# Other order and pace of the weight look-ups, half of the late reloads on GpSimd's queue, later copies of the mirrored Gram blocks

## The chip, the cores and the metric

The kernel runs on one core of one Trainium2 chip, as one launch. The metric is the device time of that launch in microseconds (us). The core has a matrix engine (TensorE, PE in the profile, with its weight loads as PEld), a vector engine (VectorE, DVE), a scalar engine (ScalarE, ACT), GpSimd (POOL) and a queue engine (SyncE, SP). SP and POOL issue the DMA transfers in this kernel.

## What is computed

The input x is 2 x 2048 x 512 in float32. Two layers follow each other, each with a layer norm ahead and the input added behind. In the attention the scores are 512 x 512: the features of q against the features of k, summed over the sequence. The second layer is a gated network whose three weight matrices are given as indices (0 to 15) into a table of 16 numbers.

```python
def attn(x, Wq, Wk, Wv, Wo):
    q, k, v = (einsum('bse,ef->bsf', x, W) for W in (Wq, Wk, Wv))
    s = einsum('bes,bfs->bef', qT, kT) / sqrt(16)
    return swapaxes(einsum('bef,bfs->bes', softmax(s), vT), 1, 2) @ Wo

def ffn(x, lut, gate_idx, up_idx, down_idx):       # 1376 x 512, 1376 x 512, 512 x 1376
    h = silu(x @ lut[gate_idx].T) * (x @ lut[up_idx].T)
    return h @ lut[down_idx].T

x = x + attn(layernorm(x), Wq, Wk, Wv, Wo)
x = x + ffn(layernorm(x), lut, gate_idx, up_idx, down_idx)
```

## The kernel before

The 4096 rows of x are eight chunks c of 512 rows, four chunks for each of the two batches; a chunk has four blocks j of 128 rows. The attention is not computed row by row: since q, k and v are linear in the normed rows n, everything comes from the Gram matrix n^T n of each batch (512 x 512). The stages, with the lines of the profile:

- **Gram stage** (`gram`, L371). For each block, ACT writes the normed rows xn (L183), and PE adds their upper Gram blocks in four banks gp. Blocks are also stored in DRAM as nd, by SP. Batch 0 ends with chunk 3. `gram_out` copies its banks to SBUF at c=4, j=1, and `gram_mirror` fills the lower blocks at c=4, j=3: six PE transposes (L432) into three banks gt, each bank followed by an ACT copy (L435). The sums of the first matrix (`left(gs[0])`) are queued in `ahead` and made by DVE from c=6 on.
- **Square stage** (L516). Products of 512 x 512 matrices, each by a Strassen-like scheme of seven half-size products, give a matrix m for each batch. The second Gram matrix is mirrored inside the first of these products.
- **y stage** (L680). For each of 32 blocks k: SP reloads nd as nl (L657), DVE transposes it 32 x 32 within rows (nT, L661), PE multiplies it by m, DVE adds the result to x (L687), ACT forms sums for the second layer norm and, six blocks later, the normed block xn_f. In block k DVE makes nT of block k+1. For blocks below 16 PE transposes xn_f (L712) to xb. The blocks from 16 on go out to DRAM (xnd, L701), come back as fl in four transfers of 64 KB by `reload` (L657), and are transposed by DVE (L661). `f_load(k)` issues the reload, `f_turned_late(k)` the transpose; they stand two blocks apart, the last of them in the next stage.
- **Gate and up stage** (L808, class `GateUp`). The hidden units are 11 tiles f of 128; the rows are four pairs p of chunks. A pass (f, p) is seven half-size products on PE, in the order a1, c1, a4 of the pass before, a2, c2, b, a3, each of four matmul records (1.72 us at full clock). DVE makes five instructions in a pass, of about 0.69 us (L128, L866, L875); SP stores each h in DRAM (hd, L831). After each of the seven products comes `between()`: it runs one item of the list `todo` (in f=0 the 20 items of late reloads, transposes and sums of xb, `f_sums`, L125), or else `pump(0.9)`.
- **Down stage** (L808, class `Down`): the same scheme with the down weights, then the sum with x and the output.

**The look-ups** are DVE work of a different kind, which the other stages carry along. There is one job for each tile f of gate and up (gu0 to gu10) and one for each two tiles of the down weights (wd0 to wd5). A job takes indices of 128 x 1024 from DRAM (`fetch`; POOL's queue from the third job on), has ACT cast them (L204), takes the bits apart (L216 to L222), and picks: eight instructions L230 and seven copy_predicated L242. A gu job ends with four sums on 128 x 256. Jobs run in one order, the list `jobs`; their index buffers are two, so the fetch of the job after next is let go by the end of a job. A gate holds job gu f (f above 1) until tile f-2 is complete. `pump(us)` adds `us` to an account and runs steps of the current job, at costs written in the code, until the account is used up:

```python
owed[0] = min(owed[0] + us, 2 * us + 1.0)
while owed[0] > 0:
    cost = next(lookup, None)
    if cost is None:
        return
    owed[0] -= cost
```

The costs of the planner are close to the profile's durations: 0.75 for L230, 1.27 for L242. At the head of tile f, whatever is missing of gu f is run at once (called a forced step in the text below):

```python
for f in range(NFT):
    while "S4" not in gu[f]:
        next(lookup)
```

The order on every engine is written out by hand (a manual schedule): an engine executes its instructions in the order in which the program emits them, and waits by semaphores.

Of the kernel before, what the change touches and what calls it, by code (L numbers as in the profile page):

```python
# [51 lines left out]
P = 128  # L52
# [6 lines left out]
def tile_attn_ffn(  # L59
# [13 lines left out]
    nc = tc.nc  # L73
# [4 lines left out]
    J = 4  # L78
    CH = J * P
    NCH = B * S // CH  # L80
    CPB = S // CH
# [3 lines left out]
    NFT = len(FT)  # L85
    NPAIR = NFT // 2
    assert E == 512 and NLUT == 16 and S % CH == 0 and NFT == 2 * NPAIR + 1
    assert B == 2 and NCH == 8
    Q = 32
# [19 lines left out]
    nd = dram.tile([NCH, J, P, E], F32, tag="nd", name="nd")  # L109
    xnd = dram.tile([NCH, J, P, E], F32, tag="xnd", name="xnd")  # L110
# [13 lines left out]
    def sub(dest, a, b):  # L124
        nc.vector.tensor_tensor(dest, a, b, ALU.subtract)  # L125

    def add(dest, a, b):
        nc.vector.tensor_tensor(dest, a, b, ALU.add)  # L128
# [122 lines left out]
    def gu_job(f):  # L251
        f0, rows = FT[f]
        n = KB * rows

        def load(queue, idx):
            queue.dma_start(idx[:, :n], gate_idx[:, KB * f0 : KB * f0 + n])
            queue.dma_start(idx[:, n:], up_idx[:, KB * f0 : KB * f0 + n])

        def dest():
            gu[f] = {  # L260
                "w": wgu.tile([P, 2, KB, P], F32, tag="w", name=f"w_{f}"),
                "s": wgu.tile([P, 3, 2, P], F32, tag="s", name=f"s_{f}"),
            }
            flat = gu[f]["w"].rearrange("p g k r -> p (g k r)")[:, : 2 * n]
            gu[f]["flat"] = flat
            return flat

        def after():
            flat = gu[f]["flat"].rearrange("p (g k r) -> p g k r", g=2, k=KB)
            a11, a12 = flat[:, 0, 0:2, :], flat[:, 0, 2:4, :]  # L270
            a21, a22 = flat[:, 1, 0:2, :], flat[:, 1, 2:4, :]
            s1, s2, s4 = (gu[f]["s"][:, q, :, :rows] for q in range(3))
            for op, d, u, v in (
                (add, s1, a21, a22), (sub, s2, s1, a11), (sub, a21, a11, a21), (sub, s4, a12, s2)
            ):
                op(d, u, v)
                yield 0.42
            gu[f].update(
                {"11": a11, "12": a12, "S3": a21, "22": a22, "S1": s1, "S2": s2, "S4": s4}
            )  # L280

        return Job(f"gu{f}", P, 2 * n, load, dest, after, lambda: f < 2 + passed[0])

    def down_job(i):
        f0, rows = FT[2 * i]
        n = 2 if i < NPAIR else 1

        def load(queue, idx):
            queue.dma_start(
                idx.rearrange("p (o e) -> p o e", o=n),  # L290
                down_idx[f0 : f0 + n * rows, :].rearrange("(o p) e -> p o e", o=n),
            )

        def dest():
            return wd[:rows, 2 * i : 2 * i + n, :].rearrange("p o e -> p (o e)")

        return Job(f"wd{i}", rows, n * E, load, dest, lambda: iter(()), lambda: True)

    jobs = [gu_job(0), gu_job(1)] + [down_job(i) for i in range(NPAIR - 1)]
    jobs += [gu_job(2), gu_job(3), down_job(NPAIR - 1), gu_job(4), gu_job(5), down_job(NPAIR)]  # L300
    jobs += [gu_job(f) for f in range(6, NFT)]

    def looked_up():

# [15 lines left out]
    def pump(us):  # L320
# [7 lines that stand above are left out]
# [26 lines left out]
    def bank(name):  # L354
        return pps.tile([P, E], F32, tag="ps", name=name, bufs=8)
# [7 lines left out]
    def gram(c, j):  # L363
        b = c // CPB
        if c % CPB == 0 and j == 0:
            gp[b] = [bank(f"gp_{b}_{i}") for i in range(KB)]
        xn = ln1[c].normed(j, xc[c][:, j, :])
        if c >= STORED:
            nc.sync.dma_start(nd[c, j], xn)
        for i in range(KB):  # L370
            nc.tensor.matmul(  # L371
                gp[b][i][:, i * P :], xn[:, i * P : (i + 1) * P], xn[:, i * P :],
                start=c % CPB == 0 and j == 0, stop=c % CPB == CPB - 1 and j == J - 1,
            )
# [11 lines left out]
    def left(t, name, order=("S2", "S4", "S1")):  # L386
        a11, a21 = t[:, 0:2, :H], t[:, 0:2, H:]
        a12, a22 = t[:, 2:4, :H], t[:, 2:4, H:]

        def s3():  # L390
            for tag in order:
                o.new(tag)
            sub(a21, a11, a21)
            o.update({"11": a11, "12": a12, "22": a22, "S3": a21})

        o = Operand(name, [
            s3, lambda: sub(o["S2"], a22, a21), lambda: sub(o["S4"], a12, o["S2"]),
            lambda: add(o["S1"], o["S2"], a11),
        ])
        return o  # L400
# [17 lines left out]
    gs = {}  # L418

    def gram_out(b):  # L420

        gs[b] = room(f"sq{b}", f"g_{b}")
        for i in range(KB):
            nc.scalar.copy(gs[b][:, i, i * P :], gp[b][i][:, i * P :])

    def gram_mirror(b):

        g = gs[b]
        for m in range(1, KB):
            ps = bank(f"gt_{b}_{m}")  # L430
            for i in range(m):
                nc.tensor.transpose(  # L432
                    ps[:, i * P : (i + 1) * P], g[:, i, m * P : (m + 1) * P], ident
                )
            nc.scalar.copy(g[:, m, : m * P], ps[:, : m * P])  # L435

    def stats1(c, *js):
        for j in js:
# [24 lines left out]
    def n_stored():  # L463
        c, j = to_store.pop(0)
        t = sums.tile([P, E], F32, tag="e", name=f"n_{c}_{j}")
        nc.sync.dma_start(nd[c, j], ln1[c].normed(j, xc[c][:, j, :], t))

    for c in range(1, NCH):
        for j in range(J):
            gram(c, j)  # L470
            if c in (CPB - 1, CPB + 1, CPB + 2):
                n_stored()
            if c + 1 < NCH and j < 2:
                for i in (2 * j, 2 * j + 1):
                    ln1[c + 1].stats(i, xc[c + 1][:, i, :])
                if j == 1:
                    ln1[c + 1].sqrt(0, J)
            elif c + 1 < NCH and j == 2:
                pump(0.6)
                ln1[c + 1].rest(0, J)  # L480
                pump(0.6)
            elif ahead and c > STORED + 2:
                for op in ahead[:4]:
                    op()
                del ahead[:4]
            else:
                pump(1.9)
            if c == 1 and j == 2:
                nc.vector.tensor_tensor(
                    lut_x, lut_pairs[:, :, 0], lut_pairs[:, :, 1], ALU.bitwise_xor  # L490
                )
            if c == CPB and j == 1:
                gram_out(0)
            if c == CPB + 1 and j == 3:
                wk_sb = load_weight(wk, "a0", "wk_sb")
                wq_sb = load_weight(wq, "a1", "wq_sb")
                wk_ops = right(wk_sb, "wk")
                ahead += wk_ops.todo
            if c == CPB and j == 3:
                gram_mirror(0)  # L500
                g_ops = [left(gs[0], "g_0")]
                ahead += g_ops[0].todo

# [67 lines left out]
    class Softmax:  # L571
# [27 lines left out]

    gram_out(1)  # L600
    g = [g_ops[0], left(gs[1], "g_1")]
    wq_ops = left(wq_sb, "wq", ("S2", "S1", "S4"))
    p1 = [room(f"a{2 + b}", f"p1_{b}") for b in range(B)]
    p1_ops = [right(p1[b], f"p1_{b}") for b in range(B)]
    assert not ahead
    square(g[0], wk_ops, p1[0], "p1_0", {
        1: [lambda: gram_mirror(1)], 4: g[1].todo[:2], 5: g[1].todo[2:],
    }, (1.2, 1.2, 1.2, 1.2, 0.3, 0.3, 1.2))
    square(g[1], wk_ops, p1[1], "p1_1", {
        3: wq_ops.todo[:2], 4: wq_ops.todo[2:], 5: p1_ops[0].todo[:2], 6: p1_ops[0].todo[2:],  # L610
# [35 lines left out]
    nls, nTs, ys, xfs, fls = {}, {}, {}, {}, {}  # L646
# [2 lines left out]
    def block(k):  # L649
        return xc[k // J][:, k % J, :]  # L650

    def reload(t, rows):

        rows = rows.rearrange("(t b) e -> b t e", b=Q)
        t = t.rearrange("p (t e) -> p t e", e=P)
        for i in range(KB):
            nc.sync.dma_start(t[i * Q : (i + 1) * Q], rows[:, :, i * P : (i + 1) * P])  # L657

    def turn(to, t):

# [5 lines left out]
    def n_load(k):  # L666
        if k < NBLK:
            nls[k] = sums.tile([P, E], F32, tag="e", name=f"nl_{k}")
            reload(nls[k], nd[k // J, k % J])

    def n_turned(k):
        if k < NBLK:
# [22 lines left out]
    EARLY = NBLK // 2  # L695
# [20 lines left out]

    def f_load(k):
        fls[k] = xnp.tile([P, E], F32, tag="xn", name=f"fl_{k}", bufs=4)
        reload(fls[k], xnd[k // J, k % J])

    def f_turned_late(k):
        turn(f_place(k), fls[k])
# [59 lines left out]
    for k in range(NBLK):  # L782
        if k:
            n_turned(k + 1)
            n_load(k + 3)
        y_product(k)
        if k == 0:
            before[0].a4()
            n_turned(1)
            n_load(2)  # L790
            n_load(3)
        else:
            side(k)
        pump(1.0 if k < EARLY + 6 else 0.5)
    pps.release()
    sums.release()
    ffn = tc.alloc_tile_pool(name="ffn", bufs=1, reuse_waits="tile")
# [319 lines left out]
    for c in range(NCH):  # L1117
        nxt = None
        for jj in range(2):
# [9 lines left out]
            u = units.pop(0)  # L1129
# [62 lines left out]
```

## Time and profile before

| | |
|---|---|
| median of 3 runs | 1124.98 us (1124.23 to 1125.58) |
| profiled execution | 1127.84 us |
| its span | 1125.7 us |
| PE busy | 1095.9 us, 97% |
| DVE busy | 696.3 us, 62% |
| ACT busy | 303.6 us, 27% |
| mean granted clock of PE | 0.991 |

The span is the profiled part of the execution; the rest of the 1127.84 us lies around it. Busy PE is not PE at its peak, since ends of matmuls are modelled. A wait is given as waiting engine and line, then what released it, then total, times and longest in us. In the timeline a line has its start, its length, the engine, the line of the kernel, the operation, and in brackets the idle time of that engine ahead of it. SPq and POOLq are the queues' own instructions.

### The profile page before, as it was taken

What the parts mean: (1) busy time and instruction counts of PE and PEld (TensorE: products, weight loads), DVE (VectorE), ACT (ScalarE), POOL (GpSimd) and SP (SyncE); (2) the same over time, 40 slices, a digit from 0 to 9 for tenths busy, and PEclk for the clock granted to TensorE, in tenths of its full rate; (3) what the DMA queues carried; (4) which work ended last, traced back from release to release, by engine and by line L of the source; (5) the groups of instructions that cost most, each with busy time, mean ns of one, the idle gap of its engine ahead of it and who ended that gap; (6) DMA issues with size and microseconds to landing.
All of it is one profiled execution on the core that took longest, in us unless ns stands there. A gap on an engine that the chain in (4) does not pass through costs nothing.

```text
span 1125.7 us, 10379 instructions
## 1 busy us (share of the span) xinstructions
PE 1095.9 (97%) x3516; PEld 656.0 (58%) x3516; DVE 696.3 (62%) x1267; ACT 303.6 (27%) x567; POOL 14.6 (1%) x31
## 2 busy tenths in 40 slices
PE   7999999999989969999999999999999999999998
PEld 4668886444434424444444444444437888888887
DVE  6887776677677778786876665855553344333341
ACT  4552522556622212222222222222221000000000
POOL 0000000000000000000000000000000000000000
PEclk9999999999999989998999999999999999999999
DMA  8371303545741111110211211101315453355420
GB/s 335 132 262 29 66 19 104 158 132 166 253 142 65 57 47 66 56 54 28 73 60 56 73 38 57 51 37 47 138 54 168 148 168 99 123 173 166 152 71 37
DMA packets 83700, 117.15 MB, mean 104 GB/s; under 512 B 16432, under 2 KB 41008, under 8 KB 81728
## 3 DMA queue, kind: packets, MB, share of 16 engines
q1 hardware_dynamic: 81456, 109.09, 28.9%
q0 software_dynamic: 2192, 7.41, 2.2%
q8 instruction: 27, 0.44, 0.2%
q14 instruction: 25, 0.20, 0.1%
HBM read 64.56 MB, written 51.90 MB: 103 GB/s over the span
## 4 chain that ended last, share of the span: by engine, by line
PE 93%; DVE 3%; SPq 1%; ACT 1%; DMA 1%; issue 1%; DVEq 0%; ACTq 0%
PE a_g L808 25%; PE a_d L808 14%; PE c_g L808 13%; PE y L680 10%; PE c_d L808 7%; PE gp L371 6%; PE b_g L808 6%; PE b_d L808 4%; PE ea_t L516 1%; SPq L657 1%; PE ea_p L516 1%; PE ea_m L516 1%; PE ea_s L516 1%; PE xt L712 1%; PE ec_t L516 1%
## 5 line engine op out<-in xcount | busy, mean ns | idle before, releaser
L128 DVE TENSOR_TENSOR c<-c_g,u 128x512 f32<-128x512 f32 (+1 forms) x44 | 30.3, 689 | 145.0 <-PE c_g L808 138.1
L680 PE MATMUL y<-m,nT 128*128 128x512 f32 x256 | 112.8, 592 | 0.0
L808 PE MATMUL a_g<-xb,w 128*128 128x512 f32 (+1 forms) x176 | 86.5, 615 | 11.8 <-DVE w L242 11.8
L808 PE MATMUL c_g<-xb,w 128*128 128x512 f32 (+1 forms) x176 | 87.0, 619 | 2.3 <-DVE xb L125 2.3
L808 PE MATMUL a_g<-xb,s 128*128 128x512 f32 (+1 forms) x176 | 82.9, 593 | 2.1 <-DVE c L128 2.1
L808 PE MATMUL a_g<-xT_a,s 128*128 128x512 f32 (+1 forms) x176 | 82.8, 593 | 0.1
L808 PE MATMUL b_g<-xb,w 128*128 128x512 f32 (+1 forms) x176 | 82.7, 592 | 0.0
L371 PE MATMUL gp<-xn_a 128*128 128x512 f32 (+3 forms) x256 | 72.6, 447 | 8.5 <-ACT xn_a L183 8.5
L680 PEld LDWEIGHTS y<-m,nT 128*128 128x128 f32 x256 | 47.4, 190 | 52.7 <-issue 52.4
L860 ACT ACTIVATE h<-h 128x512 f32<-128x512 f32 (+1 forms) x44 | 27.7, 631 | 172.8 <-DVE h L128 172.8
L808 PEld LDWEIGHTS a_g<-xb,w 128*128 128x128 f32 (+1 forms) x176 | 33.8, 194 | 56.2 <-issue 42.7
L371 PEld LDWEIGHTS gp<-xn_a 128*128 128x128 f32 x256 | 45.2, 197 | 35.7 <-issue 17.0
L808 PEld LDWEIGHTS c_g<-xb,w 128*128 128x128 f32 (+1 forms) x176 | 34.4, 196 | 48.3 <-issue 43.3
L808 PE MATMUL a_g<-xT_sq,s 128*128 128x512 f32 (+1 forms) x132 | 62.0, 592 | 0.0
L808 PEld LDWEIGHTS a_g<-xb,s 128*128 128x128 f32 (+1 forms) x176 | 33.1, 189 | 46.3 <-issue 39.0
L230 DVE TENSOR_SCALAR gu<-idx_gu,lut_x,lut_sb 128x1024 int32<-128x1024 int32 (+1 forms) x77 | 59.2, 791 | 0.0
L808 PEld LDWEIGHTS a_g<-xT_a,s 128*128 128x128 f32 (+1 forms) x176 | 32.9, 188 | 43.0 <-issue 42.0
L808 PEld LDWEIGHTS b_g<-xb,w 128*128 128x128 f32 (+1 forms) x176 | 33.0, 188 | 42.5 <-issue 42.5
L242 DVE COPY_PREDICATED gu<-b_gu,gu 128x1024 f32<-128x1024 int16 (+1 forms) x44 | 56.4, 1281 | 0.9
L808 PE MATMUL a_d<-dT,hs_a 128*128 128x256 f32 x224 | 56.2, 378 | 0.0
L242 DVE COPY_PREDICATED wd<-b_wd,wd 128x1024 f32<-128x1024 int16 (+1 forms) x42 | 50.9, 1212 | 0.8
L837 ACT COPY p<-a_g 128x512 f32<-128x512 f32 (+1 forms) x44 | 25.7, 584 | 86.0 <-PE a_g L808 86.0
(239 smaller groups left out, 1708.3 us busy)
## 6 DMA issues: line engine op xcount, KB each, us to landing
hd<-h SPq DMA_DIRECT2D x80, 256.0 KB, 2.0
h<-hd SPq DMA_DIRECT2D x40, 512.0 KB, 6.3
nl<-nd SPq DMA_DIRECT2D x128, 64.0 KB, 2.1
x1d<-x SPq DMA_DIRECT2D x8, 1024.0 KB, 4.5
r<-x1d SPq DMA_DIRECT2D x32, 256.0 KB, 4.4
out_dram<-r SPq DMA_DIRECT2D x32, 256.0 KB, 2.5
x<-in_x_dram SPq DMA_DIRECT2D x7, 1024.0 KB, 14.3
nd<-xn_a SPq DMA_DIRECT2D x20, 256.0 KB, 2.1
```

What stands on the lines that cost most here:

```text
L128: nc.vector.tensor_tensor(dest, a, b, ALU.add)
L230: vec.tensor_scalar(dest.bitcast(I32), idx, lut_x[:rows, k : k + 1], lut_i[:rows, at : at + 1], ALU.bitwise_and, ALU.bitwise_xor,)
L242: vec.copy_predicated(dest, masks[level - 1], t)
L371: nc.tensor.matmul(gp[b][i][:, i * P :], xn[:, i * P : (i + 1) * P], xn[:, i * P :], start=c % CPB == 0 and j == 0, stop=c % CPB == CPB - ...
L516: nc.tensor.matmul(ps[:, m, :], self.a[a][:, k, m * P : (m + 1) * P], self.b[b][:, k, :], start=first and m == k == 0, stop=k == 1, skip_g ...
L657: nc.sync.dma_start(t[i * Q : (i + 1) * Q], rows[:, :, i * P : (i + 1) * P])
L680: nc.tensor.matmul(ys[k], nTs[k][:, i, :], m[:, i, :], start=(i == 0), stop=(i == KB - 1))
L712: nc.tensor.transpose(ps[:, i * P : (i + 1) * P], xfs[k][:, i * P : (i + 1) * P], ident)
L808: nc.tensor.matmul(ps, lhsT, rhs, start=first and i == 0, stop=i == len(pairs) - 1, skip_group_check=not first,)
L837: nc.scalar.copy(self.p1, self.a)
L860: nc.scalar.activation(self.h0, self.h0, AF.Silu)
```

## The change

- The order of the jobs. Before: gu0, gu1, wd0 to wd3, gu2, gu3, wd4, gu4, gu5, wd5, gu6 to gu10. After: gu0, gu1, wd0 to wd2, gu2, gu3, wd3, gu4, wd4, gu5, gu6, wd5, gu7 to gu10.
- The pace in the y stage. `pump` gets 1.4 in each of the first 22 blocks, formerly 1.0, and 0.8 in the other ten, formerly 0.5. The pace in the gate and up stage remains 0.9.
- `reload` takes two queues. The first two of four transfers go to the first, the others to the second. For nl both are SP; for fl the second is POOL.
- `gram_mirror` hands back its ACT copies. For batch 0 they are run at c=5, j=1, behind the normed blocks of that step, together with the queueing of `left(gs[0])`. For batch 1 they are run one product later in the program, where ACT has nothing else in between.

```diff
-    jobs = [gu_job(0), gu_job(1)] + [down_job(i) for i in range(NPAIR - 1)]
-    jobs += [gu_job(2), gu_job(3), down_job(NPAIR - 1), gu_job(4), gu_job(5), down_job(NPAIR)]
-    jobs += [gu_job(f) for f in range(6, NFT)]
+    jobs = [gu_job(0), gu_job(1)] + [down_job(i) for i in range(3)]
+    jobs += [gu_job(2), gu_job(3), down_job(3), gu_job(4), down_job(4), gu_job(5), gu_job(6)]
+    jobs += [down_job(NPAIR)] + [gu_job(f) for f in range(7, NFT)]
...
     def gram_mirror(b):
-        g = gs[b]
+        g, copies = gs[b], []
         for m in range(1, KB):
             ps = bank(f"gt_{b}_{m}")
             for i in range(m):
                 nc.tensor.transpose(
                     ps[:, i * P : (i + 1) * P], g[:, i, m * P : (m + 1) * P], ident
                 )
-            nc.scalar.copy(g[:, m, : m * P], ps[:, : m * P])
+            copies.append(lambda d=g[:, m, : m * P], u=ps[:, : m * P]: nc.scalar.copy(d, u))
+        return copies
...
             if c == CPB and j == 3:
-                gram_mirror(0)
+                copies = gram_mirror(0)
+            if c == CPB + 1 and j == 1:
+                for copy in copies:
+                    copy()
                 g_ops = [left(gs[0], "g_0")]
                 ahead += g_ops[0].todo
...
+    copies = []
     square(g[0], wk_ops, p1[0], "p1_0", {
-        1: [lambda: gram_mirror(1)], 4: g[1].todo[:2], 5: g[1].todo[2:],
+        1: [lambda: copies.extend(gram_mirror(1))], 2: copies, 4: g[1].todo[:2], 5: g[1].todo[2:],
     }, (1.2, 1.2, 1.2, 1.2, 0.3, 0.3, 1.2))
...
-    def reload(t, rows):
+    def reload(t, rows, queues):
         rows = rows.rearrange("(t b) e -> b t e", b=Q)
         t = t.rearrange("p (t e) -> p t e", e=P)
         for i in range(KB):
-            nc.sync.dma_start(t[i * Q : (i + 1) * Q], rows[:, :, i * P : (i + 1) * P])
+            queues[i // 2].dma_start(t[i * Q : (i + 1) * Q], rows[:, :, i * P : (i + 1) * P])
...
-            reload(nls[k], nd[k // J, k % J])
+            reload(nls[k], nd[k // J, k % J], (nc.sync, nc.sync))
...
-        reload(fls[k], xnd[k // J, k % J])
+        reload(fls[k], xnd[k // J, k % J], (nc.sync, nc.gpsimd))
...
-        pump(1.0 if k < EARLY + 6 else 0.5)
+        pump(1.4 if k < EARLY + 6 else 0.8)
```

## The prediction

> **What bounds the kernel now.** I read the page's first table, then the waits of TensorE (PE), then the granted clock around each of them, then the timeline at the longest one.
>
> ```profile
> PE 1095.9 (97%) x3516; PEld 656.0 (58%) x3516; DVE 696.3 (62%) x1267; ACT 303.6 (27%) x567; POOL 14.6 (1%) x31
> ```
>
> PE is busy for 97% of the span and the change gives it no instruction less: gains and losses can only be PE's idle time and PE's slow time. Waits of PE (us in total, times, longest):
>
> ```profile
> PE a_g L808 <- DVE w L242: 11.8, 2, 9.2
> PE gp L371 <- ACT xn_a L183: 8.5, 2, 7.2
> PE c_g L808 <- DVE xb L125: 2.3, 1, 2.3
> PE a_g L808 <- DVE c L128: 2.1, 2, 1.4
> ```
>
> Row 1 is the look-up of weights finishing late, at the head of f=2 (9.19 us) and of f=4 (2.66). Row 2 is the start (7.2) and one gap of 1.28 in the Gram stage. Rows 3 and 4 lie mostly in f=0: 1.37 us at 324.5 and 2.33 at 337.4. The table of windows (stretch, length, busy PE, PEld, DVE, ACT, POOL, then the clock) adds that PE comes back from three of these at half clock:
>
> ```profile
> 337.36:340.80 3.44, 3.44 (x4) 1.41 (x5) 3.40 (x5) 0.00 (x0) 0.13 (x1) 0.52 0.20 76
> 406.88:412.40 5.52, 5.52 (x7) 2.42 (x8) 5.45 (x11) 0.59 (x1) 0.00 (x0) 0.50 0.00 0
> 508.76:514.80 6.04, 6.04 (x7) 2.52 (x8) 5.86 (x11) 0.59 (x1) 0.00 (x0) 0.50 0.05 18
> ```
>
> Half of each stretch is lost: 1.65, 2.76 and 3.02 us. After the gap of 1.37 us the clock stayed full. So the present stalls cost: Gram 1.28; f=0 1.37 + 2.33 + 1.65 = 5.35; head of f=2 9.19 + 2.76 = 11.95; head of f=4 2.66 + 3.02 = 5.68; together 24.3 us. The timeline at f=2 shows what a forced look-up costs:
>
> ```profile
> 398.08 0.68 DVE L128 TENSOR_TENSOR c<-a_g,p 128x512 f32<-128x512 f32 x1
> 398.69 0.68 DVE L866 TENSOR_TENSOR h<-h,c 128x512 f32<-128x512 f32 x1
> 399.28 0.80 DVE L230 TENSOR_SCALAR gu<-idx_gu,lut_x,lut_sb 128x1024 int32<-128x1024 int32 x1
> 400.12 1.30 DVE L242 COPY_PREDICATED gu<-b_gu,gu 128x1024 f32<-128x1024 int16 x1
> 401.31 1.53 DVE L230 TENSOR_SCALAR gu<-idx_gu,lut_x,lut_sb 128x1024 int32<-128x1024 int32 x2
> 402.87 2.62 DVE L242 COPY_PREDICATED gu<-b_gu,gu 128x1024 f32<-128x1024 int16 x2
> 405.53 1.30 DVE L242 COPY_PREDICATED w<-b_gu,gu 128x1024 f32<-128x1024 int16 x1
> ```
>
> PE had finished pass (1,3) at 397.69. DVE must first add PE's last product, then complete every outstanding step of w_2, in order; PE starts at 406.88. Nothing on PE covers these steps.
>
> **What the Trainium skill says.** "TensorE: Matmul & The Clock Gate", Part 1: PE drops to half clock after about one idle window of 3.4 us and recovers after a busy one. The trace agrees on the halving and on the length of recovery (3.4 to 6.0 us), but here gaps of 2.33 and 2.66 us were enough; the measurement decides. "DMA: Bandwidth & Descriptors", section Issuing engines are not separate DMA queues: another issuing engine saves only issue time. Here issue time is the point (below). "SBUF — State Buffer", section two separate sides: GpSimd cannot write descriptors while VectorE (DVE) is in a two-port mode. No run here shows such a block yet; this feeds the slower rival.
>
> **The change, part by part.** The base is the profiled execution, 1127.84 us with a span of 1125.7, against a median of 1124.98 (2.9 lower); I subtract the same differences from the median.
>
> 1. *Copies of the mirrored Gram blocks.* Now ACT waits 6.99 us for PE's transposes and does the copies, with the next xn behind them:
>
> ```profile
> 53.75 1.02 ACT L435 COPY g<-gt 128x128 f32<-128x128 f32 x3 [6.99 <-PE gt L432]
> 54.68 0.82 ACT L183 ACTIVATE xn_a<-x,nmr_a,rstd_a 128x512 f32<-128x512 f32 x1
> ...
> 55.54 6.63 PE L371 MATMUL gp<-xn_a 128*128 128x512 f32 x23 [1.28 <-ACT xn_a L183]
> ```
>
> In the changed order, two xn, two n and one sqrt stand ahead of the copies: 4 x 0.71 + 0.29 us from 46.8 on, the sqrt after DVE's statistics of 50.96, so done by about 51.3. The copies then wait for the transposes to 53.75 and hold up the third xn until 55.5; PE needs it after two blocks of 2.9 us, at 59.9. **-1.28**; bounds 0 to -1.3. The copies' reader is many blocks later. For the second Gram matrix the engines' order is unchanged: 0.
>
> 2. *Order and pace, y stage.* A gu job costs 8 x 0.80 + 7 x 1.31 + 0.69 + 3 x 0.42 + 4 x 0.42 = 19.2 us of DVE, a wd job 17.5. The y stage gets 35 look-up instructions for 31, all ahead of y_23. In block k DVE transposes nT of block k+1, so a late transpose is what would stop PE. In the timeline nT_19 now ends at 247.5 for a use at 249.9, nT_20 at 251.95 for 253.7: 2.3 and 1.8 us ahead. Laying the changed blocks 16 to 20 end to end (+0.2, +0.75, -0.8, +1.55 us of look-ups, the last partly into a wait of 0.33) leaves 1.4 us at nT_19 and 1.6 at nT_20 and nT_21. **0**; bounds 0 to +5 (a gap of 2 us and a slow clock of 3).
>
> 3. *Head of f=2.* The job gu2 now follows wd2 and fits into f=1: the planner gives 28 stages x 0.9 = 25.2 per f, a gu job is 18.3 in its own costs. No step is forced: **-11.95**. Each f up to 3 likewise.
>
> 4. *Head of f=4.* The last two sums of gu4 are still forced; the last copy_predicated is ahead. So a1 starts at once, and c1 waits for the third sum: 0.60 + 0.60 + 0.46 + 0.34 + 0.42 = 2.4 us after a3, against 1.72 of a1. About 0.8 us, below the 1.37 that left the clock alone: 0.8 - 5.68 = **-4.9**; if the clock halves, -1.9.
>
> 5. *Head of f=5, new.* From f=1 to f=4 come gu2, gu3, wd3, gu4, wd4, gu5: 4 x 18.3 + 2 x 16.65 = 106.6 of planner cost. There are 4 x 25.2, but gu3's gate opens only with f=2, so 6.9 of f=1 go unused, of which the account's cap returns 2 x 1.9: 97.7. The 8.9 missing are 11 forced steps of gu5: by the program's order 3 L230 and 4 L242 ahead of PE's a1, then 4 sums. Against f=2's head that is one L230 more (0.77) and 0.27 less of DVE lag: 9.7 us idle. The slow clock is 1.65 to 3.02; I take 2.5. **+12.2**; bounds 11 to 14.
>
> 6. *Reloads.* DVE waits 14.9 us in all (12 times) for fl. SP issues without a pause from 313.65 on:
>
> ```profile
> 313.65 7.31 SPq L657 DMA_DIRECT2D fl<-xnd  x12
> 321.06 0.38 SPq L831 DMA_DIRECT2D hd<-h  x1
> 321.48 3.77 SPq L657 DMA_DIRECT2D fl<-xnd  x8
> ```
>
> and ends at 329.54; the last turn starts at 331.27 and f=0's last pair of sums (L125) is late for PE. Half of it, 14 of these 28 issues, leaves SP (14 x 0.47 = 6.6 us) and goes to POOL, whose index loads show 0.54 to 0.85 us each: 14 x 0.7 = 9.8 us, landing 2.3 (SP's fl) to 3.0 (POOL's 256 KB) later, so at about 326 instead of 331.3. On POOL they stand behind gu3's index fetch, which wd2's end lets go in y_22, ahead of the first reload in y_27; wd3's fetch stands behind all 32 and is wanted only in f=2. On SP they stay behind the hd stores, which wait for DVE's h. Five us of lateness gone exceeds the 2.33 and the 1.37; DVE has 7 look-ups fewer in f=0 as well. **-5.35**; bounds 0 (nothing gained) to a loss, rival B.
>
> Sum: -1.28 + 0 - 11.95 - 4.9 + 12.2 - 5.35 = -11.3: 1116.5 for a profiled execution, **1113.7** for the median.
>
> **Rivals.** A: the reloads gain nothing, since half of each still waits behind hd on SP and the slower half decides: -11.3 + 5.35 = -5.95, **1119.0**. For it: one load of 64 KB x 4 lands no sooner than its later half. Against it: SP's unbroken issue. B, slower: POOL's descriptor writing is blocked by DVE. Now the last issue ends at 329.54; with 14 issues of d us, the lag over today is 313.65 + 14 d + 2.3 - 331.3. It eats the remaining 5.95 us from d = 1.5 us on; at 2.0 us it is +12.7, **1131.7**. Against it: the measured 0.54 to 0.85, with DVE busy, and no look-up beside the reloads in the new order. C: the y stage stops PE once (item 2, +5): **1118.7**. That a part doesn't act is item 6 at zero, so rival A.
>
> **How the numbers follow.** Forecast 0.62, A 0.20, C 0.09, B 0.07, others 0.02. The forecast's own bounds, items 4 and 5 with the clock, are 1110 to 1117; A and C bring the range to 1121.5. About 0.2%, 2.2 us, is what a measurement of this kernel can tell from no change; only A with a bad clock lands there. Faster 0.88, same 0.05, slower 0.07.
>
> **What would show it.** Right: PE's wait for w has one entry near 9.7 us at the head of f=5 (from about 536 on) and none at f=2; its gap in the Gram stage is gone; f=0 has full clock; DVE's wait for fl falls well below 14.9. Wrong: two long waits for w, a wait of PE for nT in the y stage, or POOL issues above 1.5 us.

## The result, and the profile after

The changed kernel takes 1115.47 us (median of 6 runs, 1112.96 to 1116.54), the kernel before 1123.81 us (6 runs, 1119.63 to 1125.58). The ratio is 0.9926, interval 0.9907 to 0.9946: 8.3 us, or 0.7%, faster. The profiled execution has a span of 1113.8 us, 11.9 below that of before.

The waits of PE in the changed kernel (us in total, times, longest). Lines past 296 are six later in this file; L814 is the former L808:

```profile
PE a_g L814 <- DVE w L242: 9.6, 1, 9.6
PE gp L372 <- ACT xn_a L183: 7.1, 1, 7.1
PE a_g L814 <- DVE c L128: 1.0, 2, 0.8
PE c_g L814 <- DVE w L125: 0.8, 1, 0.8
PE c_g L814 <- DVE xb L125: 0.6, 1, 0.6
```

One long wait for w is left of two. The row for gp has only the start of the kernel. Of the rows that f=0 had a part in, 0.64 us for xb and 0.17 for c remain there (the other 0.8 us for c lies at the end of the gate and up stage, as before the change), and c1 at the head of f=4 waits 0.8 us for a sum. The timeline of PE places the long wait and shows the doubled length of the four matmul records behind it:

```profile
488.69 1.98 PE L814 MATMUL c_g<-xb,w 128*128 128x512 f32 x4 [0.80 <-DVE w L125]
...
544.88 3.78 PE L814 MATMUL a_g<-xb,w 128*128 128x512 f32 x4 [9.57 <-DVE w L242]
```

This is the head of f=5. The timeline of DVE ahead of it:

```profile
535.35 0.69 DVE L128 TENSOR_TENSOR c<-a_g,p 128x512 f32<-128x512 f32 x1 [0.28 <-PE a_g L814]
535.96 0.68 DVE L872 TENSOR_TENSOR h<-h,c 128x512 f32<-128x512 f32 x1
536.55 1.53 DVE L230 TENSOR_SCALAR gu<-idx_gu,lut_x,lut_sb 128x1024 int32<-128x1024 int32 x2
538.12 1.29 DVE L242 COPY_PREDICATED gu<-b_gu,gu 128x1024 f32<-128x1024 int16 x1
539.31 1.52 DVE L230 TENSOR_SCALAR gu<-idx_gu,lut_x,lut_sb 128x1024 int32<-128x1024 int32 x2
540.87 2.63 DVE L242 COPY_PREDICATED gu<-b_gu,gu 128x1024 f32<-128x1024 int16 x2
543.53 1.30 DVE L242 COPY_PREDICATED w<-b_gu,gu 128x1024 f32<-128x1024 int16 x1
```

It is the picture of f=2 before, with one L230 more: DVE waits for PE's last product, and then runs four L230 and four L242 with nothing on PE beside them. The table of windows (stretch, length, busy PE, PEld, DVE, ACT, POOL, clock, then the DMA share and GB/s) has the slow clock behind it, about as long as the one at f=2 was:

```profile
544.88:550.40 5.52, 5.52 (x7) 2.42 (x8) 5.45 (x11) 0.58 (x1) 0.00 (x0) 0.50 0.01 3
```

In the Gram stage ACT still waits for the transposes, but the next xn are done ahead of that, and PE goes on at once (timeline of ACT and PE):

```profile
52.50 0.82 PE L433 MATMUL gt<-ident,g 128*128 128x128 f32 x6
52.81 1.02 ACT L436 COPY g<-gt 128x128 f32<-128x128 f32 x3 [1.48 <-PE gt L433]
53.16 7.07 PE L372 MATMUL gp<-xn_a 128*128 128x512 f32 x25
53.73 0.81 ACT L183 ACTIVATE xn_a<-x,nmr_a,rstd_a 128x512 f32<-128x512 f32 x1
```

The reloads by their tile (count, shortest/median/longest issue in ns), and SP's stretch that had no pause before:

```profile
L663 POOL DMA_DIRECT2D fl<-xnd x32: 549/549/566, 277.2 to 320.4; - x32
L663 SPq DMA_DIRECT2D fl<-xnd x32: 302/426/1254, 281.1 to 322.7; - x32
```

```profile
309.62 3.82 SPq L663 DMA_DIRECT2D fl<-xnd  x6
316.65 0.34 SPq L837 DMA_DIRECT2D hd<-h  x1
317.10 1.89 SPq L663 DMA_DIRECT2D fl<-xnd  x4
320.77 0.34 SPq L837 DMA_DIRECT2D hd<-h  x1
321.21 1.89 SPq L663 DMA_DIRECT2D fl<-xnd  x4
```

SP now pauses between its groups. DVE's wait for fl has fallen from 14.9 to 10.2 us.

### The profile page after: what moved, and what is told of

Same layout as the page of the kernel before. It is cut to its first block, busy times and chain, and to the rows that moved or that the text cites. A ratio compares the mean times of both kernels' runs of the same rounds, so it can differ in the third digit from the quotient of the medians.

```text
span 1113.8 us, 10427 instructions
## 1 busy us (share of the span) xinstructions
PE 1089.8 (98%) x3516; PEld 654.0 (59%) x3516; DVE 695.1 (62%) x1267; ACT 303.6 (27%) x567; POOL 32.1 (3%) x63
## 4 chain that ended last, share of the span: by engine, by line
PE 92%; DVE 3%; DMA 3%; ACT 1%; issue 1%; SPq 0%; POOL 0%; DVEq 0%; POOLq 0%; ACTq 0%
PE a_g L814 25%; PE a_d L814 14%; PE c_g L814 13%; PE y L686 9%; PE c_d L814 7%; PE gp L372 6%; PE b_g L814 6%; PE b_d L814 4%; DMA fl<-xnd 2%; PE ea_t L521 1%; PE ea_p L521 1%; PE ea_m L521 1%; PE ea_s L521 1%; PE xt L718 1%; PE ec_t L521 1%; PE ec_m L521 1%
## 5 line engine op out<-in xcount | busy, mean ns | idle before, releaser
L814 PE MATMUL a_g<-xb,w 128*128 128x512 f32 (+1 forms) x176 | 84.6, 604 | 9.6 <-DVE w L242 9.6
L814 PE MATMUL c_g<-xb,w 128*128 128x512 f32 (+1 forms) x176 | 84.1, 600 | 1.4 <-DVE w L125 0.8
L814 PE MATMUL a_g<-xb,s 128*128 128x512 f32 (+1 forms) x176 | 82.9, 593 | 1.0 <-DVE c L128 1.0
L814 PE MATMUL a_g<-xT_a,s 128*128 128x512 f32 (+1 forms) x176 | 82.8, 592 | 0.0
L814 PE MATMUL b_g<-xb,w 128*128 128x512 f32 (+1 forms) x176 | 82.7, 592 | 0.0
L814 PEld LDWEIGHTS a_g<-xb,w 128*128 128x128 f32 (+1 forms) x176 | 33.4, 191 | 53.0 <-issue 42.3
L814 PE MATMUL a_g<-xT_sq,s 128*128 128x512 f32 (+1 forms) x132 | 62.0, 592 | 0.0
L814 PEld LDWEIGHTS c_g<-xb,w 128*128 128x128 f32 (+1 forms) x176 | 33.4, 191 | 45.8 <-issue 42.2
L230 DVE TENSOR_SCALAR gu<-idx_gu,lut_x,lut_sb 128x1024 int32<-128x1024 int32 (+1 forms) x77 | 59.2, 795 | 0.0
L814 PEld LDWEIGHTS a_g<-xb,s 128*128 128x128 f32 (+1 forms) x176 | 32.8, 188 | 44.4 <-issue 38.6
L814 PEld LDWEIGHTS b_g<-xb,w 128*128 128x128 f32 (+1 forms) x176 | 33.0, 188 | 42.5 <-issue 42.5
L814 PEld LDWEIGHTS a_g<-xT_a,s 128*128 128x128 f32 (+1 forms) x176 | 32.9, 188 | 42.7 <-issue 42.0
L242 DVE COPY_PREDICATED gu<-b_gu,gu 128x1024 f32<-128x1024 int16 (+1 forms) x44 | 56.3, 1280 | 0.8
L814 PE MATMUL a_d<-dT,hs_a 128*128 128x256 f32 x224 | 56.2, 379 | 0.0
L242 DVE COPY_PREDICATED wd<-b_wd,wd 128x1024 f32<-128x1024 int16 (+1 forms) x42 | 51.0, 1215 | 0.7
```

Of the source, the lines that this page charges most:

```text
L230: vec.tensor_scalar(dest.bitcast(I32), idx, lut_x[:rows, k : k + 1], lut_i[:rows, at : at + 1], ALU.bitwise_and, ALU.bitwise_xor,)
L242: vec.copy_predicated(dest, masks[level - 1], t)
L814: nc.tensor.matmul(ps, lhsT, rhs, start=first and i == 0, stop=i == len(pairs) - 1, skip_group_check=not first,)
```

## The experiments

All times come from chips on which the kernel before ran as well; a ratio is to the kernel before on the same chip. Its median was 1122.76 us beside the first four of these kernels, 1123.20 beside all_sp, old_pace, wd4_later and old_order, 1123.76 beside all_pool, pace_f10 and old_order_f10, and 1123.81 beside the changed kernel; so a difference of two kernels from different groups is better taken from their ratios. The last columns are the sum of PE's waits in the one profile, and the middle of the mean granted clocks of the timed runs.

| kernel | median us | ratio, 95% interval | PE's waits us | clock |
|---|---|---|---|---|
| before, beside the first four | 1122.76 (26 runs) | | 25.5 | 0.994 |
| order_only | 1120.85 | 0.9987 (0.9978 to 0.9995) | 24.0 | 0.994 |
| pace_only | 1109.06 | 0.9885 (0.9869 to 0.9900) | 14.8 | 0.999 |
| reload_only | 1118.61 | 0.9966 (0.9954 to 0.9977) | 22.3 | 0.995 |
| copies_only | 1120.85 | 0.9984 (0.9974 to 0.9993) | 24.2 | 0.993 |
| changed | 1115.47 | 0.9926 (0.9907 to 0.9946) | 19.9 | 0.995 |
| all_sp | 1119.12 | 0.9964 (0.9949 to 0.9980) | 21.9 | 0.994 |
| all_pool | 1117.61 | 0.9948 (0.9933 to 0.9963) | 22.1 | 0.995 |
| old_pace | 1114.35 | 0.9923 (0.9907 to 0.9940) | 19.2 | 0.995 |
| wd4_later | 1112.97 | 0.9907 (0.9889 to 0.9926) | 16.7 | 0.997 |
| pace_f10 | 1104.69 | 0.9837 (0.9818 to 0.9855) | 11.9 | 1.000 |
| old_order | 1102.69 | 0.9819 (0.9799 to 0.9838) | 10.9 | 0.999 |
| old_order_f10 | 1101.92 | 0.9810 (0.9793 to 0.9827) | 9.4 | 1.000 |

### Each part alone, on the kernel before

**order_only**: the list of jobs as in the change, nothing else.

```diff
-    jobs = [gu_job(0), gu_job(1)] + [down_job(i) for i in range(NPAIR - 1)]
+    jobs = [gu_job(0), gu_job(1)] + [down_job(i) for i in range(3)]
...
```

> The kernel before with the new order of the jobs alone (pace 1.0 and 0.5, reloads on SP, copies as before). Theory 1, each stop of PE is priced by itself: head of f=2 gone (-11.9), head of f=4 down to a wait of 0.8 us without slow clock (-4.9), a new wait of 9.6 us plus a slow clock of about 2.7 at the head of f=5 (+12.3), the gaps of f=0 (1.4 and 2.3 us and 1.65 of slow clock) and of the Gram stage (1.28) as before: -4.5 us in sum, ratio 0.996. Theory 2, the pace is what freed the head of f=2 and the order did nothing: waits for w of 9.2 and 2.7 us at f=2 and f=4 as before, ratio 1.000. Theory 3, the order also cures f=0: -10 us, ratio 0.991.

The waits of PE:

```profile
PE a_g L808 <- DVE w L242: 9.6, 1, 9.6
...
PE c_g L808 <- DVE xb L125: 2.5, 1, 2.5
...
PE c_g L808 <- DVE w L125: 0.8, 1, 0.8
```

Theory 1 has every wait right, at the place it named: 9.6 at f=5, 0.8 at f=4, f=0 as before. Its time is not right: a ratio of 0.9987 is 1.5 us less, where 4.5 were expected. The waits alone went down by 25.5 - 24.0 = 1.5 us, so the 3 us of slow clock that were to go at f=4 are not found in the times. They are found between the two profiles, whose spans differ by 1125.7 - 1120.0 = 5.7 us; why the one profile of before has more slow clock than its usual run is taken up below. Theory 3 is out, since f=0 was not cured; theory 2 is out by the waits.

**pace_only**: the pace as in the change, nothing else.

```diff
-        pump(1.0 if k < EARLY + 6 else 0.5)
+        pump(1.4 if k < EARLY + 6 else 0.8)
```

> The kernel before with the new pace of the y stage alone (1.4 and 0.8, old order of the jobs). Theory 1: by the account of pump wd3 then ends before f=0, so that gu2 fits into f=1 and gu5 is in time too: no step of f=2 or f=5 is forced, at f=4 only the last two sums of gu4. PE waits for w nowhere, or under 1 us at f=4; f=0 and the Gram stage as before. -11.9 - 4.9 = -16.8 us, ratio 0.985: more than the whole change brought. Theory 2, rival: look-ups up to y_31 load DVE until nT or the late transposes are late, and PE waits in the y stage or longer in f=0, 5 us or more with its slow clock: ratio 0.990 or above.

Measured 0.9885, or 12.9 us, where 16.8 were expected: theory 1 in the waits, too much in the slow clock, as in order_only. This one line brings more than the whole change. The waits of PE have no row for a_g behind w L242, but two new and small ones, 1.1 us for x in f=0 and 0.8 us for w at the head of f=4:

```profile
PE c_g L808 <- DVE xb L125: 2.3, 1, 2.3
PE a_g L808 <- DVE c L128: 1.4, 2, 0.8
PE c_g L808 <- DVE x L687: 1.1, 1, 1.1
PE c_g L808 <- DVE w L125: 0.8, 1, 0.8
```

So the mechanism of theory 1 holds: with the old order, the pace lets wd3 end ahead of f=0, and neither f=2 nor f=5 has a forced copy_predicated. Theory 2 has a small part: c1 of the first pass waits 1.1 us behind DVE, which carries look-ups to y_31. In the y stage itself PE never waits. The gap of 2.3 us in f=0 is not followed by the slow clock in this profile.

**reload_only**: `reload` with two queues as in the change, nothing else.

```diff
-            nc.sync.dma_start(t[i * Q : (i + 1) * Q], rows[:, :, i * P : (i + 1) * P])
+            queues[i // 2].dma_start(t[i * Q : (i + 1) * Q], rows[:, :, i * P : (i + 1) * P])
...
-        reload(fls[k], xnd[k // J, k % J])
+        reload(fls[k], xnd[k // J, k % J], (nc.sync, nc.gpsimd))
```

> The kernel before with half of the late reloads on POOL alone. Theory 1, SP's issue time made f=0 late: DVE's wait for fl falls from 14.9 us to about 10, PE's gaps of 1.4 and 2.3 us in f=0 fall below 1 us in sum and the slow clock there is gone: -4.5 us, ratio 0.996; heads of f=2 and f=4 as before. Theory 2, the fewer look-ups of f=0 and of the last y blocks did it: gaps of f=0 as before, ratio 1.000.

PE's gaps in f=0 are 0.2 and 0.3 us, the waits for w 9.2 and 2.7 as before:

```profile
PE a_g L808 <- DVE w L242: 11.9, 2, 9.2
...
PE c_g L808 <- DVE xb L125: 0.2, 1, 0.2
```

DVE waits 9.2 us for fl. The ratio 0.9966 (3.8 us) agrees with theory 1; the look-ups in f=0 are those of before here, so theory 2 is out.

**copies_only**: `gram_mirror` and its copies as in the change, nothing else.

```diff
-                gram_mirror(0)
+                copies = gram_mirror(0)
+            if c == CPB + 1 and j == 1:
+                for copy in copies:
+                    copy()
...
```

> The kernel before with the later copies of the first mirrored Gram matrix alone. Theory 1: the one gap of 1.28 us of PE in the Gram stage is gone, all else as before: -1.3 us, ratio 0.999, which the times can hardly tell from 1; the profile decides. Theory 2: the third xn is late behind the copies in turn, and a gap of about 1 us stands two blocks later.

The row for gp is down to one entry, no gap stands two blocks later, and the other rows are those of before to within 0.2 us (L813 is L808 here):

```profile
PE a_g L813 <- DVE w L242: 11.9, 2, 9.2
PE gp L371 <- ACT xn_a L183: 7.1, 1, 7.1
```

The ratio 0.9984 (1.8 us, interval 0.8 to 2.9) agrees with 1.28.

### Parts of the changed kernel taken back

**all_sp**: in the changed kernel, fl's second queue is SP again.

```diff
-        reload(fls[k], xnd[k // J, k % J], (nc.sync, nc.gpsimd))
+        reload(fls[k], xnd[k // J, k % J], (nc.sync, nc.sync))
```

> The changed kernel with all four transfers of a late reload back on SP (new order, new pace, later copies kept). Theory 1: the gaps of f=0 come back, about 0.7 and 2.4 us, with a slow clock of 1.7 in some runs: 2.5 to 4 us above the changed kernel, some 1118.5 us. Theory 2: with no look-ups in f=0 SP's queue is no longer what is late, and the time stays at 1115.5.

1119.12 us, 3.7 above the changed kernel (4.3 by the ratios); xb is waited for 2.4 us again, and DVE waits 14.5 us for fl, as before the change. With no look-up at all in f=0 the reloads are as late as they were. Theory 1 holds.

**all_pool**: both queues POOL.

```diff
-        reload(fls[k], xnd[k // J, k % J], (nc.sync, nc.gpsimd))
+        reload(fls[k], xnd[k // J, k % J], (nc.gpsimd, nc.gpsimd))
```

> The changed kernel with all four transfers of a late reload on POOL. An issue there took 0.55 us, so 4 x 0.55 = 2.2 us for each reload against 1.1. Theory 1, the issue time of the slower queue sets when a reload lands: POOL is then as full as SP was (28 issues of the last seven reloads 15.4 us, against 13.2 on SP), f=0 is late again by 2 to 4 us: 1118 to 1119.5 us, as with all on SP. Theory 2: what delays on SP is the wait behind the hd and xnd stores, not the issue time; POOL is free of them and the time stays at 1115.5.

1117.61 us: 2.1 above the changed kernel (2.5 by the ratios), a little under theory 1's range and over theory 2's; each of its five runs is above each of the six of the changed kernel. The timeline has POOL issuing without a pause, free of hd and xnd as it is:

```profile
309.24 17.30 POOL L663 DMA_DIRECT2D fl<-xnd  x32 [1.69 <-DVE xb L667]
```

PE's gaps in f=0 sum to about 3.0 us, none followed by the slow clock. DVE's wait for fl is 10.1 us, no more than in the changed kernel, so that sum does not show the lateness. The end of the last issue does: it comes 32 us after the first product of f=0 starts, as it does in all_sp, against 33 before the change and 29 in the changed kernel. So a queue that has to issue all of the late reloads is late on either engine, as theory 1 has it. What part of SP's lateness came from hd ahead in the queue was not separated from it.

**old_pace**: the changed kernel with `pump(1.0 ... else 0.5)` in the y stage.

```diff
-        pump(1.4 if k < EARLY + 6 else 0.8)
+        pump(1.0 if k < EARLY + 6 else 0.5)
```

> The changed kernel with the old pace of the y stage (1.0 and 0.5). Theory 1: with the new order of the jobs the gates of gu2 and gu3 set what is done when, so the pace changes nothing: the same waits of 0.8 us at f=4 and 9.6 at f=5, 1115.5 us. Theory 2: the pace carries part of the gain even so, the rest of wd2 in f=0 makes f=0 late: 1118 us or more.

1114.35 us, the same waits of 0.8 and 9.6. Beside the new order the pace gives nothing. Theory 1 holds.

**old_order**: the changed kernel with the old list of jobs.

```diff
-    jobs = [gu_job(0), gu_job(1)] + [down_job(i) for i in range(3)]
+    jobs = [gu_job(0), gu_job(1)] + [down_job(i) for i in range(NPAIR - 1)]
...
```

> The changed kernel with the old order of the jobs (new pace, split reloads, later copies kept). Theory 1: no wait for w but 0.8 us at f=4, no gap in the Gram stage, f=0 below 1 us but for about 1 us where c1 of its first pass waits for DVE: 1109.1 of the pace alone - 1.3 - 2.9 - 1 of slow clock, some 1104 us, ratio 0.983. Theory 2: the look-ups that stand up to y_31 press DVE while POOL writes descriptors, f=0 is late again: 1108 or more.

1102.69 us, ratio 0.9819: theory 1, a little under its number. These are the largest waits of PE:

```profile
PE gp L372 <- ACT xn_a L183: 7.0, 1, 7.0
PE a_g L814 <- ACT p L843: 1.3, 1, 1.3
PE c_g L814 <- DVE w L125: 0.8, 1, 0.8
PE a_g L814 <- DVE c L128: 0.8, 1, 0.8
PE a_d L814 <- DVE r L128: 0.5, 1, 0.5
```

No long wait but the start is left. The new order of the look-ups therefore costs the change about 12 us (1115.47 - 1102.69 = 12.8; 12.0 by the ratios). DVE's timeline shows how: in the changed kernel it makes no look-up from 261.7 us, the end of wd2, to 343.2, the end of f=0. The next job is gu2, which its gate holds until tile 0 is complete, and wd3, which has no such gate, stands behind it. In old_order wd3 goes on in that time: ten look-up instructions more in the y stage (46 for 36) and six for one in f=0.

### What the wait at f=5 is made of

**wd4_later**: the changed kernel with gu5 and wd4 exchanged.

```diff
-    jobs += [gu_job(2), gu_job(3), down_job(3), gu_job(4), down_job(4), gu_job(5), gu_job(6)]
+    jobs += [gu_job(2), gu_job(3), down_job(3), gu_job(4), gu_job(5), down_job(4), gu_job(6)]
```

> The changed kernel with one pair of jobs exchanged: gu5 ahead of wd4. Theory 1: by the account nothing of gu5 is then forced; at f=4 the last two sums are forced as in the changed kernel, at f=6 the four sums, at f=7 the last copy_predicated and the sums. So the wait of 9.6 us and its slow clock go (-12.3), waits of about 2.6 us come at f=6 and 3 to 4 at f=7, each with up to 3 us of slow clock: about 1108 to 1113 us. Theory 2, the rival: the missing DVE time only moves, and the sum of waits for w stays near 10 us in one place: 1115 us.

1112.97 us. The timeline of PE has the two waits where the account put them:

```profile
586.00 2.60 PE L814 MATMUL a_g<-xb,w 128*128 128x512 f32 x4 [2.59 <-DVE w L242]
...
639.41 3.78 PE L814 MATMUL a_g<-xb,w 128*128 128x512 f32 x4 [3.39 <-DVE w L242]
```

The first is the head of f=6, the second of f=7. The wait of 9.6 us is gone and 6.0 have come in its place: the account of `pump` tells which head is late, and by how much.

**pace_f10**: the changed kernel with the pace of the gate and up stage raised.

```diff
         else:
-            pump(0.9)
+            pump(1.0)
```

> The changed kernel with the pace of the gate and up stage at 1.0 for 0.9. Theory 1, DVE has the time and only the account withholds it: by the account six steps stay forced at the head of f=5, four sums and the next job's first two, none at f=4; the wait of 9.6 us becomes one of about 2.6, with a slow clock of 1.7 to 3: 9 us less than the changed kernel, some 1106 us. Theory 2: a pass can't hold 7 us of look-ups beside its five other instructions, DVE falls behind and PE waits in many passes: no gain, 1114 us or more.

1104.69 us: theory 1. The wait at f=5 is 2.66 us, as worked out, without the slow clock in this profile. So DVE had the time, and the shortage was in the account.

**old_order_f10**: old order, all other parts of the change, and 1.0 for 0.9.

```diff
-    jobs = [gu_job(0), gu_job(1)] + [down_job(i) for i in range(3)]
+    jobs = [gu_job(0), gu_job(1)] + [down_job(i) for i in range(NPAIR - 1)]
...
-            pump(0.9)
+            pump(1.0)
```

> The old order of the jobs with the other parts of the change, and in addition 1.0 for 0.9 in the gate and up stage. Theory 1: no step is forced anywhere, the wait of 0.8 us at f=4 goes, some 1101.9 us. Theory 2: DVE is too full in some passes and waits of PE for c or h take its place: 1103 or more.

1101.92 us, ratio 0.9810, the fastest of all: 13.5 us under the changed kernel (13.0 by the ratios). The wait at f=4 is gone, and no wait for c or h has come up beside those known: 0.7 us for p at f=0, and the 0.8 us for c near the end of the gate and up stage that the kernel before has as well.

## Why the prediction was right

The sum was -11.3 us from the profiled execution; its span fell by 11.9 and the medians by 8.3. That the spans come so near is in part luck: of their 11.9 us, PE's waits are 5.6 and its slow clock 4.7 (half of 15.35 us of work at half clock before, less half of 5.92 after), and 1.6 us belong to no item. Point by point:

- **Item 1, copies.** Predicted -1.28; PE's gap is gone, in the change and in copies_only. Right.
- **Item 2, y stage.** Predicted 0; PE has no wait there in the changed kernel or in any of the eleven of the experiments. Right. But the prediction took the pace only for its risk. It did not run the account once with the new pace and the old order. That would have said what pace_only shows: the pace alone frees the head of f=2.
- **Item 3, head of f=2.** No wait is left. The reason given, that gu2 now follows wd2, is sufficient (order_only, old_pace) and not the only one (pace_only).
- **Item 4, head of f=4.** Predicted a wait of 0.8 us of c1 and no slow clock; measured 0.80, full clock. Right in the wait.
- **Item 5, head of f=5.** Predicted 9.7 us idle and 2.5 of slow clock; measured 9.57, and half clock for the 5.52 us shown and 0.4 us beyond, that is 3.0. Right.
- **Item 6, reloads.** Predicted -5.35 with nothing left; 0.17 and 0.64 us of gaps remain, without slow clock. The mechanism, SP's issue time, is shown by reload_only and all_sp. POOL's issues took 0.55 us where 0.7 was taken, and the median time from issue to landing of fl rose from 2.3 us to 3.1 over both queues.

The mis-sized term is the slow clock of the kernel before. The prediction subtracted 2.76 + 3.02 + 1.65 = 7.4 us (7.7 by the clock records) from one profile, and then the same difference from the median. That profile's mean clock was 0.991. In the 41 timed runs of the kernel before on the two chips of the first four kernels and of all_sp, old_pace, wd4_later and old_order it was 0.991 to 0.996, and the time went with it: 1119.57 us at 0.996, 1126.46 at 0.991. One thousandth of 1123 us is 1.1 us; from 0.991 to the usual 0.994 are 3.4 us, and the shortfall is 11.3 - 8.3 = 3.0. PE's waits tell the rest: they fell by 25.5 - 19.9 = 5.6 us against 6.3 predicted (1.28 + 9.19 + 2.66 - 0.8 - 9.7 + 3.7), while for the clock 8.3 - 5.6 = 2.7 us are left for 4.9 predicted. The profile of before thus has as much slow clock as this kernel showed in any run, and the median could not lose what most runs do not have. The last section shows why the runs differ.

Rival A (reloads bring nothing) fell by reload_only. Rival B (POOL blocked, from 1.5 us an issue) fell by the 549 to 566 ns of its 32 issues, with transposes and sums on DVE beside them; in old_order, where L230 and L242 ran beside a few of them as well, they took 552 to 568 ns. Rival C (the y stage stops PE) did not occur.

## What to carry to other kernels

When work for a later stage is paced by an account, run the account through to the end for each part of a change on its own. Here the order of the jobs only moved a stop of 9 us from one tile to another, since it put a job that has to wait at a gate ahead of one that has not, and the pace without it was worth more than everything together. Look for the instruction whose end releases the matrix engine and count what stands between its last input and it: forced steps behind the engine's own last product are covered by nothing. Subtract from a median only what a median has, since a stop of two to three us costs its slow clock in some runs and not in others.

## What was not expected of the hardware

The slow clock after a short gap of PE is not a matter of its length alone. By the profiles of the thirteen kernels, gaps up to 1.4 us were never followed by it. Gaps of 2.12, 2.32, 2.35 and once 2.66 us were not either. A gap of 2.33 us was, and so were 2.54, 2.59, 3.39, and 2.66 us in three other profiles; after 9.2 to 9.6 us it came each time.

The clock records of the profiles show what decides. Within a run, half clock begins and ends only at whole multiples of 3.41 us from its other beginnings and ends: before the change it begins at 337.50, 402.35 and 508.16 us, which are 19 and 31 such windows apart. The idle time of PE inside one window is what counts. In all thirteen profiles, each window at full clock with 2.06 us or more of it was followed by half clock, and none with 1.98 us or less. Two gaps of 2.66 us show it; the first two lines are the head of f=4 before the change, the others the head of f=5 in pace_f10 (its windows are counted back from the half clock that begins at 1102.45):

```profile
504.75:508.16 3.41, 1.35 (x4) 0.28 (x2) 3.41 (x5) 0.63 (x1) 0.00 (x0) 1.00 0.20 77
508.16:511.57 3.41, 2.81 (x4) 1.26 (x5) 3.34 (x9) 0.00 (x0) 0.00 (x0) 0.50 0.20 77
532.43:535.84 3.41, 1.43 (x4) 0.36 (x2) 3.41 (x5) 0.63 (x1) 0.00 (x0) 1.00 0.20 77
535.84:539.25 3.41, 2.73 (x7) 1.30 (x8) 3.34 (x9) 0.58 (x1) 0.00 (x0) 1.00 0.23 82
```

PE is idle for 3.41 - 1.35 = 2.06 us of the first window and for 1.98 us of the third. Where the windows lie differs from run to run, so the same gap can cost its slow clock in one run and not in another: pace_only, whose gap of 2.32 us in f=0 is spread over two windows (1.41 and 0.91) in its profile, has a mean clock of 1.000 in two runs and of 0.998 in two. The profile of before has six windows at half clock. Each takes 3.41 / 2 / 1125.7 = 0.0015 off the mean clock, so the 0.994 of the usual run stands for about four; this is an estimate, since the timed runs have only their mean clock on record. The ends of PE's matmuls are modelled, so the bound near 2 us is no sharper than that model.

POOL's issue of a transfer of 64 KB took 0.55 us, with DVE's transposes, sums and look-ups beside it, against a median of 0.43 on SP.
